# A four-layer network on one core: router weights held in TensorE, slot places made by POOL, and nine latent pieces a unit instead of eight

## The chip, the core and the metric

The kernel runs on one NeuronCore of a Trainium2 chip. The metric is the device time of one execution in microseconds (us); the figure for a kernel is the median of its runs. Engines are named as the profile names them: PE is TensorE (PEld its weight loads), DVE is VectorE, ACT is ScalarE, POOL is GpSimd, SP is SyncE, which here issues nearly all plain DMAs.

## The reference, cut to what matters

A network of four layers works on `x` of 4 x 512 tokens with 256 features, all in float32. Each layer normalises `x` and adds an attention part and a feed-forward part to it. The change touches layer 2 alone. Its attention part is a gated linear attention (16 heads); its feed-forward part is a small transformer block of its own: a latent attention, then a mixture of experts with one shared expert and seven routed ones, of which each token takes two.

```python
x = x + _L2_attn_ref(xn, ...) + _L2_ffn_ref(xn, ...)      # xn = layernorm(x)

def expert_ffn(x, wg, wu, wd):
    h = silu(x @ wg) * (x @ wu) / 8.0
    return h @ wd

def moe(x, sh_gate, sh_up, sh_down, r_gate, r_up, r_down, router_w, router_b):
    shared = expert_ffn(x, sh_gate, sh_up, sh_down)
    logits = x @ router_w + router_b                      # 256 -> 7
    probs = sigmoid(logits)
    scores, idx = top_k(probs, 2)
    scores = scores / sum(scores)
    w = sum(one_hot(idx, 7) * scores)
    return shared + sum over e of w[e] * expert_ffn(x, r_gate[e], r_up[e], r_down[e])

h = x + attention(rmsnorm(x, ln1_w), ...)                 # the latent attention
out = h + moe(rmsnorm(h, ln2_w), ...)
```

## The kernel before, in words

**Data.** The stream `x` and its normalised rows `xn` stay on the chip: 16 tiles of 128 tokens, 4 to a batch of 512. A batch transposed to features (two blocks of 128 features by 512 tokens) is made by `to_features`. A float32 product appears in the trace as two records on PE, a transpose as one.

**Who orders the instructions.** The program is written as generators that are advanced in turn, and a scheduler then fixes one order for each engine: it takes instructions by priority (their place in the written program) when its own estimates say that their inputs and buffers are ready, so neighbouring pieces are mixed. On the chip each engine runs its list in that order and waits at the first instruction whose inputs are not there. Pools give each tile name a number of buffers; an instruction that writes a new tile waits until the old user of the buffer has finished.

**Layer 2.** `layer2` runs 32 gated units (8 pairs of heads x 4 batches). `run(u, beside, rate)` advances three chains of one unit: `gated_unit` (scores `sc`, values `pt` with Wv, sums `st`, `pok`, the turned products `okt` and `pvt`, gates `pt` with Wg, the second scores, `pov`), `gated_supply` for the next unit (projections `pj` with Wk, Ws, Wq and the turned copies `turn`) and `gated_drain` for the unit before (`ot`, then `o` with Wo). After each of its 19 steps it adds `rate` to a credit that begins at zero in each call, and advances another chain, `beside`, once for every whole credit:

```python
credit = 0.0
for what in "mmmmsmsmmdmmsmsdmsd":
    next(chains[what], None)
    credit += rate
    while credit >= 1:
        credit -= 1
        next(beside, None)
```

For units 0 to 23 (`first` is 24) the chain beside is `latent_chain`, the whole latent attention and the router, at the rate `beside`. After unit 23 whatever is left of it is written in one go. For units 24 to 31 it is `routed2`, at the rate 1.25: the dispatch of tokens to experts, then 38 blocks of 128 rows through four stages (`fetch2`, `features2`, `hidden2`, `output2`).

**The latent chain** goes over 16 groups of heads (4 batches x 4) with three groups in flight: `latent_inputs` per batch, `latent_keys`, `latent_maxima` (scores `qk`, their maxima `mx`), `latent_va` per batch, `latent_values` (scores `kq`, exponentials `pr`, masks by POOL, `pv`, `pvt`), then per batch `latent_output` (`att`, `op`) and `experts2`.

**`experts2`** adds `h` to `x` on POOL (L1616), normalises it (squares on ACT, rsqrt on POOL, the scaling L1448 on DVE), transposes it to `a2T`, and computes the router's logits `lg`: for each of four tiles of tokens the 128 tokens are the stationary operand and the 7 columns of router weights stream by (L1626, two blocks of features), and the bias comes in as a product of a row of ones with the bias row (L1629). Then come the sigmoid (L1632), the two best by `top_weights`, their shares, and in the next piece the shared expert: `gu` (L1643), SiLU (L1646), the product (L1647), and `down` (L984).

**`dispatch`** turns the choices of all 2048 tokens into places. PE counts (`rank` L171, `count` L173); DVE makes each token's slots. The table from slot to token is built by PE: for each of 16 tiles and 2 choices, `place` (L239, 128x128, one where a lane equals the place inside the block) and `token` (L241, 128x38) are made, and `in_slot` (L244) accumulates `place` transposed times `token`. `place` and `token` have four buffers each. Then POOL gathers each block's rows by an indirect DMA (`r`, L294), SP loads the expert's weights `we`, and POOL sends the results back by an indirect DMA (`l_outs`, L334). The same `dispatch` serves layer 3.

**Around it on POOL.** The scaling of a gated unit's result `o` is three POOL instructions: a sum (L1301), a power (L1305) and the product in two halves (L1308). They stand in the same in-order list as the masks (L1558), the rsqrt steps (L377, L378) and the indirect DMAs.

Of the kernel before, what the change touches and what calls it, by code (L numbers as in the profile page):

```python
# [7 lines left out]
F32 = mybir.dt.float32  # L8
AF = mybir.ActivationFunctionType
ALU = mybir.AluOpType  # L10
# [3 lines left out]
P = 128  # L14
NB = 4
T = 512
D = 256
KD = D // P
NTILE = NB * T // P
EXT = 272  # L20
NEG = -3.0e38
# [16 lines left out]
def of_parity(ap, p):  # L38

    return ap.rearrange("q (j two) -> q two j", two=2)[:, p, :]  # L40
# [38 lines left out]
class Net:  # L79
# [78 lines left out]
    def dispatch(self, moe, rows, top, w, wk, pool, tag, keep=None):  # L158
# [3 lines left out]
        nc = self.nc  # L162
        ne, k, blocks = moe["ne"], moe["k"], moe["blocks"]
        cols = NTILE * ne
        tile = lambda name, *shape, dt=F32, of=wk: of.tile(list(shape), dt, tag=name, name=name, bufs=1)
# [62 lines left out]
        inside, first, less = tile("inside", P, NTILE, k), tile("first", P, NTILE, k), tile("less", P, NTILE)  # L228
# [6 lines left out]
        ps = pool.tile([P, blocks], F32, tag=tag, name="in_slot")  # L235
        for i in range(NTILE):
            for m in range(k):
                place = wk.tile([P, P], F32, tag="place", name="place", bufs=4)
                nc.vector.tensor_scalar(place, self.lane, inside[:, i, m : m + 1], None, ALU.is_equal)  # L239
                token = wk.tile([P, blocks], F32, tag="token", name="token", bufs=4)  # L240
                nc.vector.tensor_scalar(  # L241
                    token, self.starts[:, :blocks], first[:, i, m : m + 1], less[:, i : i + 1], ALU.is_equal, ALU.mult
                )
                nc.tensor.matmul(  # L244
                    ps, place, token, start=(i == m == 0), stop=(i == NTILE - 1 and m == k - 1)
                )
            if i % 2:
                yield
# [742 lines left out]
    def layer2(self):  # L991

        nc, a = self.nc, self.a
        UNITS = 8 * NB

        first, beside = 24, 0.44
        moe = self.moe2
        with ExitStack() as ctx:  # L1000
            tp = lambda n, bufs, **k: ctx.enter_context(self.tc.tile_pool(name=n, bufs=bufs, **k))
            self.gp = gp = {"wk": tp("ga", 1), "wk2": tp("ga2", 2), "ps": tp("gaps", 4, space=PSUM)}
            gp["gn"] = gn = gp["wk"].tile([P, 1], F32, tag="gn", name="gn")
            self.load(gn, a["l2_gn"])
            weights, units = self.weights, {}

            def supplied(u):
                pair, b = u // NB, u % NB
                for _ in norms[b]:
                    pass  # L1010
                if pair not in weights:
                    weights[pair] = self.gated_weights(pair)
                units[u] = {"b": b, "w": weights[pair]}
                return self.gated_supply(units[u])

            def normed(b):
                self.layer_norm(b)
                yield
                self.to_features(
                    gp["ps"], self.xn[:, 4 * b : 4 * b + 4, :], self.xnT[:, :, b * T : (b + 1) * T], tag="ps"  # L1020
                )
                yield

            def run(u, beside, rate):


                supply = supplied(u + 1) if u + 1 < UNITS else iter(())
                drain = self.gated_drain(units[u - 1]) if u else iter(())
                credit = 0.0
                chains = {"m": self.gated_unit(units[u]), "s": supply, "d": drain}  # L1030
# [7 lines that stand above are left out]
            norms = [normed(b) for b in range(NB)]  # L1038
            for it in (norms[0], supplied(0)):
                for _ in it:  # L1040
                    pass
            with ExitStack() as lctx:
                lp = self.lp
                lp["wk"] = lctx.enter_context(self.tc.tile_pool(name="la", bufs=1))
                lp["w"] = lctx.enter_context(self.tc.tile_pool(name="laps", bufs=4, space=PSUM))
                latent = self.latent_chain()
                for u in range(first):
                    run(u, latent, beside)
                for _ in latent:
                    pass  # L1050
            wk = tp("ex", 4)
            gp["ex"] = tp("exps", 4, space=PSUM)
            routed = self.routed2(wk)
            for u in range(first, UNITS):
                if u == UNITS - 1:
                    for _ in routed:
                        pass
                    self.collect(moe, wk)
                run(u, routed, 1.25)
            for _ in self.gated_drain(units[UNITS - 1]):  # L1060
                pass
        self.held.close()
# [280 lines left out]
    def latent_ahead(self, wp):  # L1343

        nc, a, NR = self.nc, self.a, 7
# [1 line left out]
        kvq, rk, up = tile("kvq", P, KD, P), tile("rk", P, KD, T), tile("up", P, 2, T)  # L1347
        vu, ow, ln1, shift_row = tile("vu", 64, D), tile("ow", P, KD, D), tile("ln1", P, D), tile("shift_row", P, 1)
        rotk, rotq = tile("rotk", P, T), tile("rotq", P, 2, T)
        rw, rb, ln2, sh = tile("rw", P, KD, NR), tile("rb", 1, NR), tile("ln2", P, D), tile("sh", P, 3, D)  # L1350
        kp = lambda ap: ap.rearrange("(k p) n -> p k n", p=P)
        self.load(kvq, kp(a["l2_kvq"]))
        self.load(ln1, a["l2_ln1"].partition_broadcast(P))
# [9 lines left out]
        self.load(ow, kp(a["l2_o_w"]))  # L1363
        self.load(shift_row, a["shift_row"])
        self.load(rw, kp(a["l2_rw"]))
        self.load(rb, a["l2_rb"])
        self.load(ln2, a["l2_ln2"].partition_broadcast(P))
        for q, n in enumerate(("gate", "up")):
            self.load(sh[:, q].rearrange("p (k i) -> p k i", k=KD), kp(a["l2_sh_" + n]))
# [238 lines left out]
    def experts2(self, b):  # L1608

        nc, lp = self.nc, self.lp  # L1610
        NR = 7
# [7 lines left out]
        aT = wk.tile([P, KD, T], F32, tag="a1", name="a2T")  # L1619
        self.to_features(pw, h, aT, tag="w")  # L1620
        yield
        ps = pw.tile([P, 4, NR], F32, tag="w", name="lg")
        for i in range(4):
            c, p = i // 2, i % 2
            for k in range(KD):
                nc.tensor.matmul(  # L1626
                    ps[:, i, :], of_parity(aT[:, k, c * D : (c + 1) * D], p), rw[:, k, :], start=(k == 0), stop=False
                )
            nc.tensor.matmul(ps[:, i, :], self.ones_row, rb, start=False, stop=True)  # L1629
        pr = self.small.tile([P, 4, NR + 6], F32, tag="pr", name="pr", bufs=2)  # L1630
        nc.gpsimd.memset(pr, NEG)
        nc.scalar.activation(pr[:, :, :NR], ps, AF.Sigmoid)  # L1632
        yield
        top, _ = self.top_weights(pr, NR, 2)
        nc.vector.tensor_copy(self.top2[:, 4 * b : 4 * b + 4, :NR], top)
        nc.vector.tensor_tensor(top, top, pr[:, :, :NR], ALU.mult)
        self.share(self.w2[:, 4 * b : 4 * b + 4, :NR], top)

        ps = []
        for q in range(2):  # L1640
# [5 lines left out]
        nc.scalar.activation(u, ps[0], AF.Silu)  # L1646
        nc.vector.scalar_tensor_tensor(u, ps[1], 1.0 / 8, u, ALU.mult, ALU.mult)  # L1647
        yield
        self.down(b, lambda cs: [u[:, cs]], [sh[:, 2, :]], None, pw, "w")
        yield  # L1650

# [255 lines left out]
```

## Time and profile before

| what | value |
| --- | --- |
| median of 3 runs | 2368.2 us (2363.25 to 2370.14) |
| the profiled execution | 2364.41 us, of which the span is 2362.7 us |
| PE / DVE / ACT / POOL busy | 2024.8 / 1249.7 / 831.7 / 622.3 us |
| chain that ended last, by engine | PE 61%, DVE 13%, issue 12%, DMA 7%, POOL 5% |
| layer 2, first gated unit to the first `sc` of unit 24 | 568 to 1560 us |
| dispatch of layer 2, `rank` to the last `in_slot` | 1597 to 1625 us |
| end of the last gated unit's last `o` (L1328) | 1916 us |

The profile is one execution. Busy shares are averages over stages that have different limits; the row of forty slices gives the busy share in tenths for 59 us each, and the row of the clock what PE was granted. A busy PE is not PE at its peak: records of matmuls overlap, and their ends are modelled. An idle time is put down to the one who ended it.

### The profile page before, as it was taken

What the parts mean: (1) busy time and instruction counts of PE and PEld (TensorE: products, weight loads), DVE (VectorE), ACT (ScalarE), POOL (GpSimd) and SP (SyncE); (2) the same over time, 40 slices, a digit from 0 to 9 for tenths busy, and PEclk for the clock granted to TensorE, in tenths of its full rate; (3) what the DMA queues carried; (4) which work ended last, traced back from release to release, by engine and by line L of the source; (5) the groups of instructions that cost most, each with busy time, mean ns of one, the idle gap of its engine ahead of it and who ended that gap; (6) DMA issues with size and microseconds to landing.
All of it is one profiled execution on the core that took longest, in us unless ns stands there. A gap on an engine that the chain in (4) does not pass through costs nothing.

```text
span 2362.7 us, 36356 instructions
## 1 busy us (share of the span) xinstructions
PE 2024.8 (86%) x13455; PEld 1500.8 (64%) x13455; DVE 1249.7 (53%) x3747; ACT 831.7 (35%) x1708; POOL 622.3 (26%) x725
## 2 busy tenths in 40 slices
PE   5754087876999999999999999999999868998985
PEld 2452076763666676666666676667788656777884
DVE  5755066658556655555556555637556575223222
ACT  1110056652334433434434333442444323333211
POOL 5324534443121211121121212112343231112221
PEclk9855599997999999999999999988999979999998
DMA  9911378873000000000000000003333305445675
GB/s 313 326 40 64 122 265 274 273 262 119 1 12 5 10 12 6 7 10 5 8 10 5 12 5 5 17 1 123 110 102 103 114 19 179 162 161 189 218 258 202
DMA packets 152537, 244.03 MB, mean 103 GB/s; under 512 B 15846, under 2 KB 111944, under 8 KB 152232
## 3 DMA queue, kind: packets, MB, share of 16 engines
q1 hardware_dynamic: 137336, 199.50, 25.9%
q0 software_dynamic: 15024, 42.20, 5.2%
q8 instruction: 107, 1.75, 0.3%
q14 instruction: 70, 0.57, 0.1%
HBM read 190.41 MB, written 66.58 MB: 109 GB/s over the span
## 4 chain that ended last, share of the span: by engine, by line
PE 61%; DVE 13%; issue 12%; DMA 7%; POOL 5%; ACT 2%; SPq 1%; POOLq 0%; another core or an unknown queue 0%; DVEq 0%; ACTq 0%
PE pt L1215 7%; PE pj L1137 6%; PE o L1328 4%; DMA r<-l_rows,in_slot 3%; PE g L1717 3%; PE kq L1550 3%; PE pov L1279 3%; PE sc L1200 2%; PE gu L958 2%; PE qk L1518 2%; PE o L1727 2%; DVE junk L1525 2%; PE pv L1566 2%; PE o L971 1%; POOL l_outs L334 1%
## 5 line engine op out<-in xcount | busy, mean ns | idle before, releaser
L334 POOL DMA_INDIRECT l_outs<-y,to x172 | 169.5, 986 | 383.6 <-ACT y L333 292.5
L1717 PE MATMUL g<-rT,we 128*128 128x128 f32 x1248 | 157.8, 285 | 8.0 <-ACT rT L327 7.7
L1717 PEld LDWEIGHTS g<-rT,we 128*128 128x128 f32 x1248 | 153.4, 200 | 15.4 <-ACT rT L327 12.5
L333 ACT ACTIVATE y<-o,share 128x256 f32<-128x256 f32 x172 | 80.9, 473 | 195.3 <-PE o L1727 108.3
L1525 DVE CUSTOM_DVE_ANT_0 junk<-qk,hide 128x512 f32<-128x512 f32 (+3 forms) x256 | 124.6, 487 | 43.5 <-PE qk L1518 24.9
L294 POOL DMA_INDIRECT r<-l_rows,in_slot x77 | 76.8, 998 | 244.8 <-PE rt L325 158.2
L306 DVE TENSOR_TENSOR mine<-r,number 128x2 f32<-128x2 f32 (+1 forms) x96 | 16.3, 170 | 227.0 <-DMA r<-l_rows,in_slot 164.3
L1558 POOL TENSOR_SCALAR_AFFINE_SELECT pr<-pr 128x512 f32<-128x512 f32 x64 | 40.2, 639 | 338.6 <-ACT pr L1555 338.6
L958 PE MATMUL gu<-rT,we 128*128 128x128 f32 x760 | 111.6, 286 | 19.3 <-issue 9.5
L1328 PE MATMUL o<-Wo,oT 128*128 128x256 f32 x512 | 125.2, 387 | 0.0
L1215 PE MATMUL pt<-Wg,xnT 128*128 128x256 f32 x512 | 123.2, 392 | 1.7 <-ACT oT L1322 0.7
L958 PEld LDWEIGHTS gu<-rT,we 128*128 128x128 f32 x760 | 103.5, 197 | 31.3 <-issue 15.2
L325 PE MATMUL rt<-ident,r 128*128 128x128 f32 x344 | 65.4, 296 | 67.6 <-DMA r<-l_rows 62.9
L1215 PE MATMUL pt<-Wv,xnT 128*128 128x256 f32 x512 | 120.1, 386 | 0.0
L1206 DVE TENSOR_TENSOR s<-sc,keep 128x512 f32<-128x512 f32 x128 | 82.4, 683 | 70.5 <-PE sc L1200 70.5
L1150 DVE RECIPROCAL rz<-rz 128x128 f32<-128x128 f32 x128 | 117.4, 935 | 0.4
L327 ACT COPY rT<-rt 128x256 f32<-128x256 f32 x172 | 61.4, 372 | 148.7 <-PE rt L325 79.4
L1215 PEld LDWEIGHTS pt<-Wg,xnT 128*128 128x128 f32 x512 | 96.3, 194 | 25.9 <-issue 7.1
L410 PE MATMUL tr<-ident,xn 128*128 128x128 f32 x160 | 34.2, 353 | 85.6 <-DVE xn L395 81.0
L1215 PEld LDWEIGHTS pt<-Wv,xnT 128*128 128x128 f32 x512 | 95.0, 191 | 14.9
L1555 ACT ACTIVATE pr<-kq 128x512 f32<-128x512 f32 (+1 forms) x192 | 86.2, 530 | 49.9 <-PE kq L1550 49.4
L1328 PEld LDWEIGHTS o<-Wo,oT 128*128 128x128 f32 x512 | 97.2, 200 | 8.7 <-ACT oT L1322 0.2
(455 smaller groups left out, 4505.2 us busy)
## 6 DMA issues: line engine op xcount, KB each, us to landing
we<-l_packed SPq DMA_DIRECT2D x133, 384.0 KB
we<-l_w SPq DMA_DIRECT2D x78, 512.0 KB
we<-l_wo SPq DMA_DIRECT2D x39, 512.0 KB
l_rows<-none SPq DMA_DIRECT2D x1, 12920.0 KB
r<-l_rows SPq DMA_DIRECT2D x19, 680.0 KB
xn<-l_outs SPq DMA_DIRECT2D x32, 256.0 KB
l_rows<-xn SPq DMA_DIRECT2D x8, 544.0 KB
l_packed<-l_w_gate SPq DMA_DIRECT2D x1, 4096.0 KB
```

Of the source, the lines that this page charges most:

```text
L294: self.nc.gpsimd.indirect_dma_start(out=r[:, m, :], out_offset=None, in_=moe["rows"][:, :], in_offset=bass.IndirectOffsetOnAxis(ap=moe["in ...
L333: nc.scalar.activation(y, ps, AF.Copy, scale=share)
L334: self.no_order(moe["name"] + " back", nc.gpsimd.indirect_dma_start(out=moe["outs"][:, :], out_offset=bass.IndirectOffsetOnAxis(ap=to, axi ...
L958: nc.tensor.matmul(ps[:, q, :], we[:, q, k * P : (k + 1) * P], rT[:, k, :], start=(k == 0), stop=(k == KD - 1))
L1137: nc.tensor.matmul(ps, w[n][:, k, :], self.xnT[:, k, t["b"] * T : (t["b"] + 1) * T], start=(k == 0), stop=(k == KD - 1))
L1150: inverse = lambda c: nc.vector.reciprocal(rz[:, c * P : (c + 1) * P], rz[:, c * P : (c + 1) * P])
L1206: nc.vector.tensor_tensor(s, ps[hh], keep4, ALU.mult)
L1215: nc.tensor.matmul(ps[:, i, :], self.xnT[:, k, s : s + P], w[n][:, k, :], start=(k == 0), stop=(k == KD - 1))
L1328: nc.tensor.matmul(ps[:, p, :], of_parity(oT[:, h, c * D : (c + 1) * D], p), wo[:, h, :], start=(h == 0), stop=(h == 1),)
L1525: nc.vector.tensor_tensor_reduce(out=junk[:, :m], in0=tiles[j][:, off : off + m], in1=self.hide[:, T - m :], op0=ALU.add, op1=ALU.max, sca ...
L1555: nc.scalar.activation(pr[:, j, off : off + m], tiles[j][:, :m], AF.Exp, scale=0.25)
L1717: nc.tensor.matmul(pt[:, m, :], we[:, q, k * T + m * P : k * T + (m + 1) * P], rT[:, k, :], start=(k == 0), stop=(k == KD - 1),)
```

## The change

Four things are done, all in layer 2.

1. In `layer2` the rate of the latent chain beside units 0 to 23 goes from 0.44 to 0.475.
2. In `experts2` the router's logits are computed with the router weights as the stationary operand: `lgT` has 7 rows and 512 token columns. ACT copies it out of PSUM and adds the bias, which for that is loaded as a column of 7 instead of a row. Four transposes then bring it back to tokens by 7.
3. The pieces of `experts2` are cut anew: the logits now stand in one piece with the shared expert's `gu`, SiLU and product; transposes and sigmoid are the next piece; the choice of the two best stands with `down`. There are five pieces as before.
4. In `dispatch`, `place` is made by POOL for layer 2. Layer 3's stays on DVE.

```diff
         for i in range(NTILE):
             for m in range(k):
                 place = wk.tile([P, P], F32, tag="place", name="place", bufs=4)
-                nc.vector.tensor_scalar(place, self.lane, inside[:, i, m : m + 1], None, ALU.is_equal)
+                (nc.gpsimd if moe is self.moe2 else nc.vector).tensor_scalar(place, self.lane, inside[:, i, m : m + 1], None, ALU.is_equal)
...
-        first, beside = 24, 0.44
+        first, beside = 24, 0.475
...
-        rw, rb, ln2, sh = tile("rw", P, KD, NR), tile("rb", 1, NR), tile("ln2", P, D), tile("sh", P, 3, D)
+        rw, rb, ln2, sh = tile("rw", P, KD, NR), tile("rb", NR, 1), tile("ln2", P, D), tile("sh", P, 3, D)
...
-        self.load(rb, a["l2_rb"])
+        self.load(rb, a["l2_rb"].rearrange("o n -> n o"))
...
-        ps = pw.tile([P, 4, NR], F32, tag="w", name="lg")
-        for i in range(4):
-            c, p = i // 2, i % 2
-            for k in range(KD):
-                nc.tensor.matmul(
-                    ps[:, i, :], of_parity(aT[:, k, c * D : (c + 1) * D], p), rw[:, k, :], start=(k == 0), stop=False
-                )
-            nc.tensor.matmul(ps[:, i, :], self.ones_row, rb, start=False, stop=True)
-        pr = self.small.tile([P, 4, NR + 6], F32, tag="pr", name="pr", bufs=2)
-        nc.gpsimd.memset(pr, NEG)
-        nc.scalar.activation(pr[:, :, :NR], ps, AF.Sigmoid)
-        yield
-        top, _ = self.top_weights(pr, NR, 2)
-        nc.vector.tensor_copy(self.top2[:, 4 * b : 4 * b + 4, :NR], top)
-        nc.vector.tensor_tensor(top, top, pr[:, :, :NR], ALU.mult)
-        self.share(self.w2[:, 4 * b : 4 * b + 4, :NR], top)
+        ps = pw.tile([NR, T], F32, tag="w", name="lgT")
+        for k in range(KD):
+            nc.tensor.matmul(ps, rw[:, k, :], aT[:, k, :], start=(k == 0), stop=(k == KD - 1))
+        lg = wk.tile([NR, T], F32, tag="q1", name="lgT")
+        nc.scalar.activation(lg, ps, AF.Identity, bias=rb)

         ps = []
         for q in range(2):
...
         nc.scalar.activation(u, ps[0], AF.Silu)
         nc.vector.scalar_tensor_tensor(u, ps[1], 1.0 / 8, u, ALU.mult, ALU.mult)
         yield
+        ps = pw.tile([P, 4, NR], F32, tag="w", name="lg")
+        for i in range(4):
+            c, p = i // 2, i % 2
+            nc.tensor.transpose(ps[:, i, :], of_parity(lg[:, c * D : (c + 1) * D], p), self.ident[:NR, :NR])
+        pr = self.small.tile([P, 4, NR + 6], F32, tag="pr", name="pr", bufs=2)
+        nc.gpsimd.memset(pr, NEG)
+        nc.scalar.activation(pr[:, :, :NR], ps, AF.Sigmoid)
+        yield
+        top, _ = self.top_weights(pr, NR, 2)
+        nc.vector.tensor_copy(self.top2[:, 4 * b : 4 * b + 4, :NR], top)
+        nc.vector.tensor_tensor(top, top, pr[:, :, :NR], ALU.mult)
+        self.share(self.w2[:, 4 * b : 4 * b + 4, :NR], top)
         self.down(b, lambda cs: [u[:, cs]], [sh[:, 2, :]], None, pw, "w")
         yield
```

`lgT` in SBUF takes the buffer `q1`, which the keys (`latent_keys`) and the maxima (`latent_maxima`) use too.

## The prediction

> **What bounds the kernel now.** I began with the page: the busy shares, the forty slices, and the clock granted to PE.
>
> ```profile
> span 2362.7 us, 36356 instructions
> PE 2024.8 (86%) x13455; PEld 1500.8 (64%) x13455; DVE 1249.7 (53%) x3747; ACT 831.7 (35%) x1708; POOL 622.3 (26%) x725
> PE   5754087876999999999999999999999868998985
> PEclk9855599997999999999999999988999979999998
> ```
>
> From slice 10 to slice 31 PE is full, and this is the gated layer; no other engine is. So within the layer a change is worth what it takes from PE: its work, its idle time, and its time at a lower clock. The dip of the clock row in slices 26 and 27 (1536 to 1654 us) is where the change acts. The second view is the table of stretches (width, then busy time of PE, PEld, DVE, ACT, POOL, then granted clock, DMA share, GB/s).
>
> ```profile
> 570.00:1540.00 970.00, 960.68 (x6636) 651.11 (x6635) 570.53 (x1354) 383.89 (x709) 161.41 (x184) 0.98 0.03 8
> 1540.00:1560.00 20.00, 16.99 (x131) 10.58 (x129) 6.98 (x18) 6.08 (x15) 6.31 (x8) 0.91 0.00 1
> 1560.00:1576.00 16.00, 16.00 (x93) 11.24 (x92) 3.34 (x6) 7.37 (x19) 2.68 (x4) 0.79 0.00 0
> 1576.00:1592.00 16.00, 14.48 (x59) 8.63 (x57) 4.69 (x26) 7.47 (x13) 2.74 (x3) 0.79 0.00 1
> 1592.00:1608.00 16.00, 14.75 (x93) 10.38 (x92) 12.92 (x53) 5.59 (x9) 0.37 (x3) 1.00 0.00 1
> 1608.00:1626.00 18.00, 16.86 (x92) 14.53 (x92) 15.98 (x74) 0.59 (x1) 0.31 (x1) 0.78 0.37 125
> 1626.00:1644.00 18.00, 15.34 (x93) 13.46 (x94) 10.83 (x47) 4.75 (x12) 11.39 (x12) 0.78 0.56 180
> 1700.00:1800.00 100.00, 99.19 (x710) 81.01 (x709) 60.40 (x185) 47.11 (x99) 42.75 (x44) 1.00 0.34 104
> ```
>
> The 970 us before 1540 lose 1% to idle PE and 2% to the clock; so nearly does the stretch after 1700. Between them lies the seam: the latent pieces left over after unit 23, then the dispatch of layer 2. There PE idles 9.6 us in 104 (3.0 + 0 + 1.5 + 1.3 + 1.1 + 2.7) and the clock falls. The third view says who was waited for in the seam (total us, times, longest), and two rows of PE in order of time say what the lower clock costs: the same 32 matmuls take 2.36 us at clock 1.00 and 4.14 us at 0.50, a ratio of 1.75.
>
> ```profile
> PE o L1106 <- DVE h L1101: 2.3, 1, 2.3
> PE pv L1566 <- POOL pr L1558: 2.3, 1, 2.3
> PE tr L410 <- DVE xn L1448: 1.5, 1, 1.5
> ```
>
> ```profile
> 1511.59 2.36 PE L1566 MATMUL pv<-pr,va 128*32 128x512 f32 x32
> 1563.24 4.14 PE L1566 MATMUL pv<-pr,va 128*32 128x512 f32 x32
> ```
>
> The last view is the rows of single lines (min/median/max ns), from which the moved operations are priced.
>
> ```profile
> L239 DVE TENSOR_SCALAR place<-lane,inside x32: 278/282/290, 1608.7 to 1623.8; 128x128 f32<-128x128 f32 x32
> L241 DVE TENSOR_SCALAR token<-starts,first,less x32: 297/299/302, 1608.3 to 1624.0; 128x38 f32<-128x38 f32 x32
> L1558 POOL TENSOR_SCALAR_AFFINE_SELECT pr<-pr x64: 633/634/798, 638.6 to 1563.8; 128x512 f32<-128x512 f32 x64
> L377 POOL TENSOR_SCALAR rms<-ms x8: 193/193/487, 545.4 to 1577.6; 128x4 f32<-128x4 f32 x8
> L1305 POOL TENSOR_TENSOR rs<-rs,neghalf x32: 1633/1644/1674, 611.7 to 1907.9; 128x8 f32<-128x8 f32 x32
> ```
>
> **The rate 0.44 to 0.475.** The latent chain has 208 pieces (12 inputs, 16 keys, 64 maxima, 4 va, 80 values, 12 outputs, 20 router and shared expert). The credit starts at zero in every unit, so 19 steps give floor(8.36) = 8 pieces now and floor(9.025) = 9 after. 24 units place 192 now; 16 are left, and they are the last values, the output and the whole router of batch 3, each waiting for the one before it. With 9 a unit, 207 are placed by unit 22 and the last one in unit 23. In the built program's order the last shared expert's `o` moves from the middle of unit 24 to the start of unit 23, and from the first matmuls of unit 25 on PE's order is the same, instruction for instruction. So the whole effect is how soon PE comes to unit 25.
>
> What can be had: idle 9.6 less the usual 1% (1.0) is 8.6 us. The clock: 20 x 0.09 + 32 x 0.21 + 36 x 0.22 = 16.4 us of (1 - clock), so 33 us at half, less the usual 2% of 104 us (4 at half): 29 x (1 - 1/1.75) = 12.3 us. Together 20.9.
>
> What stays: units 23 and 24 now run with little beside them. Two gated units are 55 us of PE (about 27.6 each, summing one unit's rows), and with shared `o`, rank, count, in_slot and two expert blocks some 75. The stretch 1592:1608 shows such a lone unit: 1.25 us idle in 16, so 5.9 in 75, less 0.7 usual, 5.2. One fall of the clock, 6.8 us long like that of 1560 to 1567, is 2.9. The second `op` of batch 3 stands only 4.3 us of PE ahead of the transposes `tr`, while add, squares, rsqrt and scale need about 5.7 (0.7 + 2.5 + 1.2 + 0.4 and handovers): a wait of 1.5, already counted within the 5.2. So 8 stays, from 3 to 20.9.
>
> The clock can be read in two ways. In this trace it fell to 0.50 at 1560 though PE had idled only 0.3 us since 1554, and at 1622 in a run of narrow matmuls with no gap at all; I therefore count the clock as tied to how full PE's work is, and the seam's loss as recoverable. The Trainium skill, "TensorE: Matmul & The Clock Gate", in "Why this matters for your kernels", ties a fall to idle gaps over about 3 us. No gap in the seam is that long (the longest is 2.4 us), so by that rule the seam should not have lost its clock, and the gain from clock would be zero and not 12.3.
>
> **The router.** Now 12 products per batch: 24 records of 128x7 (859.45 to 862.93 us, 3.5 us of PE), each bound by its weight load of 0.19 us. After: two products of 512 columns, four records like `pj` (1.98 us), and four transposes (0.6 us, like the four of `okt`): 2.5 us. Saved 1.0 x 4 = 4 us. ACT gets one more pass of 128x512 size, 0.6 us x 4, at 41% load; its chain (matmul, ACT, transpose, sigmoid) is longer, but `rank` stands some 15 us of PE behind the last transposes. The Sigmoid's table load stays. The bias tile is one DMA at 126 us in place of another, used 480 us later: nothing. Putting the router behind the shared expert keeps five pieces per batch: nothing by itself.
>
> **The places on POOL.** 32 `place` leave DVE, about 0.2 us each in its pipeline, 6.6 us. No row shows this operation on POOL. Ends: 0.19 (L377, 128x4) and 1.64 us (L1305, the slow power). I take 0.3, between L377 and the 128x512 select at 0.63, since the size lies between and the kind is L377's. POOL's order is four places, unit 23's three-step scaling of `o` (3.9 us), then 28 places, then the gathers of rows, which need all 32 anyway. The `token`s wait for buffers that `in_slot` frees, and behind them on DVE stand `ke`, `ok`, `mx` of unit 24, for which PE waits: a slow POOL would stop all three. The cover: among the 28 places' matmuls PE has 9.6 us of unit 24 (`st` 0.57, `pj` 1.98 twice, `pok` 1.96, `okt` 0.66, `st` 0.88, `ot` 1.09, part of `Wg` 0.46) and 28 x 0.39 = 10.9 of its own `in_slot` work: 20.5 us. At 0.3 POOL needs 8.4, all hidden; PE pays from 20.5 / 28 = 0.73 us per place. The fifth place comes about 13.6 us after the end of the `sc` before it (dispatch ops on DVE 5.0, `o` and `ms` 2.5, POOL 4.2, products 1.6, one place) and PE asks for it after about 13.8: 0 to 2 us late, I take 0. As PE's `in_slot` is bound by its weight loads (64 x 0.19 = 12.3 us) the relief of DVE gains PE nothing: 0.
>
> The rule against this move is in the Trainium skill, "SBUF — State Buffer", "Who interferes with whom": a DVE `tensor_scalar` in its two-port mode and a POOL instruction lock each other out. No row before shows such a pair. If each place waited for a token, it would cost an estimated 0.6 us, 16.8 in all, still under the cover, and the sum would not change.
>
> **Sum.** 20.9 + 4.0 - 8.0 = 16.9, taken as 17 us. The profiled execution took 2364.4 us (span 2362.7), so 2347; it lies 3.8 below the median of the runs, 2368.2, so the median after is 2351.
>
> **Rivals.** (A) The seam only moves. Units 23 and 24 lose as the stretch 1626:1644 does: 0.148 idle per us and clock 0.78. Over 75 us that is 11.1 + 33 x (1 - 1/1.75) = 25 us, as much as is removed: about 2368. For it: a dispatch inside a lone unit is the same in both. Against: 1592:1608 lost no clock, and the `in_slot` matmuls are now mixed with wide ones. (B) Slower: POOL's places are slow. At L1305's 1.64 us they take 45.9, which is 25.4 over the cover: net +8.5, 2377. It decides from (20.5 + 17) / 28 = 1.34 us per place. Against: only the power has such a row. (C) The change doesn't do what it says: nine pieces a unit make PE wait for DVE more often than the seam did (now 5.9 us in 13 waits of `kq` for `mx`); four times that takes the gain away, 2369. Against: DVE is at 59%.
>
> **How the numbers follow.** My case 0.74, A 0.15, B 0.07, C 0.04. About 0.3% (7 us, so 2361 and 2375) is what a measurement of this kernel can tell from no change. My case lies below 2361, with an eighth of A: faster 0.76; the rest of A and half of C: 0.15; B and half of C: 0.09. My case alone: from 24.9 (nothing stays) to 8 us of gain, 2343 to 2360. The range adds 5 us below, for runs as far below the median as the fastest shown, and reaches above into A: 2338 to 2366.
>
> **What would show it.** Right: clock near 1.00 and idle under 8 us between the last `att` (L1593) and unit 25; `lgT` of about 2 us; `place` on POOL under 0.73 us with no wait of `in_slot` for it; unit 25 some 17 us earlier and all later stages moved as a block. Wrong: the fall of the clock found again around `in_slot`; DVE idle for buffers of `token`; PE's idle between 570 and 1540 risen by more than 10 us.

## The result, and the profile after

The kernels before and after were compared in 20 runs each. After takes 2370.4 us (median), before 2375.3; the ratio of after to before is 0.9986, 95% interval 0.9969 to 1.0004. Three to five microseconds, not clear of zero, came out of a forecast of 17. The kernel before itself has medians between 2358 and 2375 us on the chips used here, so in what follows only ratios on one chip, and parts of a trace, are compared.

The page of the profiled execution of after, the rows of PE as before (the span is 2383.4 us):

```profile
PE 2036.2 (85%) x13391; PEld 1504.8 (63%) x13391; DVE 1248.7 (52%) x3715; ACT 835.8 (35%) x1711; POOL 642.5 (27%) x757
PE   6654178865999999999999999999999879998985
PEclk9855599997999999999999999999999977999997
```

The dip of the clock row that stood in slices 26 and 27 is gone: the seam was closed as forecast. But PE's busy time rose by 11 us, though the router now takes less of it. The stretches say where (columns as before: width, busy PE, PEld, DVE, ACT, POOL, clock, DMA):

```profile
574.00:1535.00 961.00, 941.55 (x6343) 627.87 (x6345) 548.44 (x1327) 376.70 (x698) 159.03 (x184) 0.97 0.02 7
...
1600.00:1620.00 20.00, 18.02 (x128) 14.89 (x126) 17.16 (x64) 3.54 (x7) 13.43 (x21) 1.00 0.34 113
1620.00:1640.00 20.00, 18.85 (x136) 14.48 (x135) 13.88 (x39) 7.68 (x12) 12.40 (x19) 1.00 0.18 55
```

From 1540 to 1640, with all of the dispatch in it, the clock is 1.00. The loss stands ahead of it, in the weave, as the units with the latent chain beside them are called from here on: in 961 us of it PE idles 19.5 us, where 970 us of before had 9.3. The waits of PE in 574 to 1655 (total us, times, longest) name most of it:

```profile
PE kq L1550 <- DVE mx L1525: 10.8, 18, 2.4
PE pt L1215 <- DVE pv L1254: 3.1, 4, 1.0
```

The same wait in before (565 to 1680):

```profile
PE kq L1550 <- DVE mx L1525: 5.9, 13, 1.6
```

The scores `kq` waited for the maxima 13 times before (5.9 us) and 18 times now. That was rival C. These waits are 4.9 of the 11 us of new idle time; the gates `pt`, which wait for `pv`, add 2.7 (0.4 before). And idle time is only half of the loss. One row of the `qk` matmuls by shape (count, covered time, which is the time with at least one of them on PE, mean ns of one, idle before them), of before and then of after, shows equal count and equal mean but more time covered; the other three shapes of `qk` rise too (18.3 to 20.5, 11.4 to 14.0 and 9.4 to 11.9 us):

```profile
L1518 PE MATMUL qk<-kT,q 32*128 32x384 f32 x128 | 21.2, 533 | 0.3 <-DVE mx L1525 0.3
```

```profile
L1518 PE MATMUL qk<-kT,q 32*128 32x384 f32 x128 | 25.3, 533 | 0.0
```

The four matmuls of a score piece use 32 rows of the array each, and run side by side when all four PSUM banks are free; when the banks come free one after the other they start one after the other. No row of waits shows that time, for PE counts as busy. Two `qk` pieces of the same 16 records in after, in order of time, are such a pair: 1.15 us, and 2.26 us beside the exponentials (ACT, 807.19 to 809.25) that empty its banks.

```profile
762.01 1.15 PE L1518 MATMUL qk<-kT,q 32*128 32x384 f32 x16
808.17 2.26 PE L1518 MATMUL qk<-kT,q 32*128 32x384 f32 x16
```

In the first piece the four heads start within 0.02 us. In the second they start 0.15, 0.49 and 0.49 us apart, the last three each 0.05 us after an exponential has ended. Before has such pieces too, but fewer: 5 of the 16 `qk` pieces of this kind cover over 1.5 us there, 10 in after.

The Trainium skill, "TensorE: Matmul & The Clock Gate", "Part 3: Packing small matmuls — row/col tiling", says that matmuls in different row groups overlap; the fast piece agrees (1.15 us), and the slow one shows what the overlap needs here.

**The account.** The stage from the first `sc` of unit 0 to the first `sc` of unit 26 holds the same work in both kernels, but for the router. It took 1112.8 us in the profile of before, 1119.5 in a second one, 1119.4 in after. Against the second one, whose clock was lower in the weave too, the gains are: idle in the seam (from unit 22 on) 12.3 to 8.9, 3.4 us; time at half clock (granted clock 0.50) there 34 to 0, at the 1.75 of the prediction 14.6 us; the router's rows 16.8 to 10.3, 6.5 us. Together 24.5. The losses: idle in the weave (units 0 to 21) 8.2 to 19.4, 11.3 us; covered time of `qk`, `kq` and `pv` 183.8 to 196.0, 12.2 us; clock in the weave (45.5 to 51.6 us at half) 2.6. Together 26.1. The stage should be 1.6 longer and is 0.1 shorter. The clock's part of the loss is the least certain. In the weave the three executions with the rate 0.475 (after, a_again and rate_only below) spent 48 to 57 us at half clock, the five with eight pieces at the old places 19 to 46; between the means, 52.1 and 30.6, lie 21.5 us, which at 1.75 is 9.2 us rather than 2.6. Why the clock falls there was not tested.

### The profile page after: what moved, and what is told of

It is laid out like the page before. It is cut to its first block, busy times and chain, and to the rows that moved or that the text cites. A ratio compares the mean times of both kernels' runs of the same rounds, so it can differ in the third digit from the quotient of the medians.

```text
span 2383.4 us, 36271 instructions
## 1 busy us (share of the span) xinstructions
PE 2036.2 (85%) x13391; PEld 1504.8 (63%) x13391; DVE 1248.7 (52%) x3715; ACT 835.8 (35%) x1711; POOL 642.5 (27%) x757
## 3 DMA queue, kind: packets, MB, share of 16 engines
q8 instruction: 107, 1.75, 0.3%
## 4 chain that ended last, share of the span: by engine, by line
PE 61%; DVE 12%; issue 11%; DMA 5%; SPq 4%; POOL 4%; ACT 2%; another core or an unknown queue 0%; POOLq 0%; DVEq 0%; ACTq 0%
PE pt L1215 8%; PE pj L1137 6%; SPq L356 4%; PE o L1328 4%; PE g L1718 4%; PE kq L1550 3%; PE gu L958 3%; DMA r<-l_rows,in_slot 3%; PE sc L1200 2%; PE pov L1279 2%; PE o L1728 2%; PE qk L1518 2%; PE o L971 2%; PE pv L1566 2%; DVE junk L1525 1%
## 5 line engine op out<-in xcount | busy, mean ns | idle before, releaser
L1718 PE MATMUL g<-rT,we 128*128 128x128 f32 x1248 | 161.9, 289 | 7.8 <-ACT rT L327 7.8
L1328 PE MATMUL o<-Wo,oT 128*128 128x256 f32 x512 | 131.8, 403 | 0.0
L1328 PEld LDWEIGHTS o<-Wo,oT 128*128 128x128 f32 x512 | 101.0, 207 | 18.3 <-issue 4.0
L1555 ACT ACTIVATE pr<-kq 128x512 f32<-128x512 f32 (+1 forms) x192 | 86.9, 530 | 54.9 <-PE kq L1550 54.6
```

Of the source, the lines that this page charges most:

```text
L1328: nc.tensor.matmul(ps[:, p, :], of_parity(oT[:, h, c * D : (c + 1) * D], p), wo[:, h, :], start=(h == 0), stop=(h == 1),)
L1555: nc.scalar.activation(pr[:, j, off : off + m], tiles[j][:, :m], AF.Exp, scale=0.25)
L1718: nc.tensor.matmul(pt[:, m, :], we[:, q, k * T + m * P : k * T + (m + 1) * P], rT[:, k, :], start=(k == 0), stop=(k == KD - 1),)
```

## The experiments

All are from the same two sources. Idle is PE's in 575 to 1495 us (920 us less busy time); the next column is the covered time of `qk`, `kq` and `pv` up to unit 26; the stage is that of the account. "Short" counts how often the gated PE work between a `qk` piece and the `kq` piece behind it is under 2 us, in 575 to 1495 of the trace.

| kernel | pieces a unit, placed | idle us | qk+kq+pv us | short | stage us | ratio to before (95%) |
| --- | --- | --- | --- | --- | --- | --- |
| before; b_again | 8, credit | 8.8; 8.8 | 183.1; 183.8 | 0; 0 | 1112.8; 1119.5 | 1 |
| after; a_again | 9, credit | 19.5; 19.4 | 196.0; 196.0 | 9; 9 | 1119.4; 1120.0 | 0.9986; 0.9998 (0.9979–1.0017) |
| rate_only | 9, credit | 19.5 | 197.9 | 9 | 1130.3 | 1.0049 (1.0032–1.0066) |
| rest_only | 8, credit | 9.0 | 183.8 | 0 | 1108.2 | 0.9973 (0.9955–0.9991) |
| router_only | 8, credit | 9.0 | 183.6 | 0 | 1111.9 | 0.9997 (0.9982–1.0011) |
| pool_only | 8, credit | 8.9 | 183.2 | 0 | 1116.5 | 0.9999 (0.9985–1.0013) |
| even | 8.67, carried | 25.3 | 182.5 | 7 | 1114.0 | 0.9993 (0.9976–1.0009) |
| placed9; again | 9, fixed steps | 11.1; 11.1 | 182.9; 183.5 | 5; 5 | 1100.8; 1103.7 | 0.9901 (0.9881–0.9922); 0.9935 (0.9917–0.9954) |
| short8 | 8, fixed steps | 19.2 | 204.3 | 9 | 1144.5 | 1.0138 (1.0116–1.0160) |
| placed_only; again | 9, fixed steps | 11.1; 11.0 | 183.8; 183.9 | 5; 5 | 1119.8; 1119.8 | 1.0006 (0.9994–1.0018); 1.0015 (0.9998–1.0033) |
| banks_a | 9, credit | 33.1 | 172.9 | 9 | 1130.6 | 1.0109 (1.0089–1.0129) |
| first26 | 8, credit | 9.1 | 177.3 | 0 | – | 0.9935 (0.9912–0.9958) |

### The parts of the change

b_again and a_again are the two kernels unchanged; rate_only is before with 0.475, rest_only after with 0.44, router_only before with the new `experts2`, pool_only before with the places on POOL. Each is a part of the diff shown above, for instance

```diff
-  first, beside = 24, 0.44      # rate_only, from before
+  first, beside = 24, 0.475
```

> The kernel before once more, for a second profile: how far the stage from the first gated unit to unit 25 varies between executions (1066.9 us in the first profile, 9.4 us of idle PE before the seam). Theory W (weave: nine latent pieces a unit bring PE to the score matmuls before DVE has read the PSUM banks of the last ones, so PE waits and the four row groups no longer run side by side): again 1067 +- 6 us, idle in the weave 8 to 11, and `kq` waits for `mx` under 7 us. Theory N (noise: the profiled execution of the changed kernel was a bad one): the stage moves by 10 us or more between executions of one kernel.

> The changed kernel once more. W: the stage from the first gated unit to unit 25 again takes 1070 to 1085 us, with 18 to 23 us of idle PE before 1540, `kq` waiting for `mx` 9 to 12 us, and `qk` busy 70 us or more instead of 60; the time within 0.4% of before. N: that stage is shorter than before's by 10 to 17 us in this execution, and the time is 10 us or more below before's or lost behind unit 25.

> The kernel before with the rate 0.475 alone. W: the seam is gone (PE full and clock 1.00 around the last `att`), but the weave has the idle time of the changed kernel (18 to 23 us before 1540) and `qk` busy 70 us or more: time within 6 us of before, 3 to 5 us above the changed kernel (its router is missing). Theory P (POOL's places, 0.6 us each, eat the gain): 8 us or more faster than the changed kernel, since no place is on POOL. N: 13 to 17 us faster than before.

> The changed kernel with the rate 0.44: router and POOL's places alone. W: idle in the weave back at 8 to 11 us and `qk` busy 60 us, the seam of 16 late pieces is back with its falls of the clock; time 2 to 6 us below before, from the router. P: slower than before by 3 to 8 us, as POOL's places stand bare in the seam. N: 3 to 5 us below before.

> The kernel before with the router part alone (rate 0.44, places on DVE). If the 4 us that the prediction gave to the router are right and the places on POOL are worth nothing: 3 to 6 us below before, and within 3 us of the kernel with router and places (1108 us for the stage, 0.27% below before). If the places on POOL bring part of that: no more than 2 us below before.

> The kernel before with the places on POOL and nothing else. The prediction put this at zero: place 0.6 us each on POOL (as in after), hidden, ratio 0.998 to 1.002, unit 24 to unit 26 within 3 us of before's 125. Rival: taking 32 places off DVE, which is busy 0.9 of the time during in_slot, makes in_slot faster: then this part is what rest_only (0.9973) has over router_only (0.9997), ratio 0.996 to 0.998.

The idle time and the lost overlap in the weave belong to the rate and to nothing else: rate_only has 19.5 us of idle like after, rest_only and router_only 9.0. They come back alike in each of the executions, so they are no accident of one profile. The rate alone makes the kernel 0.3 to 0.7% slower, where its term of the sum was a gain of 12.9 us. The places on POOL are worth nothing by themselves, as forecast; the router's 4 us (0.17%) lie inside its interval. Together, in rest_only, they gain 0.27%, which is clear of zero; rest_only also has the least time at half clock in the weave (19 us, for 27 to 46 in the other four with eight pieces), and whether its gain is more than that is open.

### Slow readers or few banks?

half_a and half_b are after and before with half of the columns of each maximum left out; the exponentials are scaled so that they stay finite:

```diff
-  out=junk[:, :m], in0=tiles[j][:, off : off + m], in1=self.hide[:, T - m :],
+  out=junk[:, : m // 2], in0=tiles[j][:, off : off + m // 2], in1=self.hide[:, T - m : T - m // 2],
...
-  nc.scalar.activation(pr[:, j, off : off + m], tiles[j][:, :m], AF.Exp, scale=0.25)
+  nc.scalar.activation(pr[:, j, off : off + m], tiles[j][:, :m], AF.Exp, scale=0.0001)
```

> The changed kernel with each maximum of the latent scores taken over the first half of its columns only (DVE's 256 instructions of L1525 shrink from about 490 to 300 ns), and the exponentials scaled to stay finite; all else as it was, and PE's order nearly so. Theory W (PE comes to the score matmuls before DVE has read their PSUM banks): the wait of `kq` for `mx` falls from 10.8 us to under 5, `qk` + `kq` + `pv` are busy 184 to 188 us instead of 196, idle PE in the weave falls from 19 to under 13, and the stage from the first gated unit to unit 26 falls from 1120 to 1095 to 1107 us. Theory R (the denser weave costs PE through its clock or through the order of matmuls alone, not through DVE): the stage stays within 5 us of 1120.

> The kernel before with the same halved maxima. W: less to free here, since its wait of `kq` for `mx` is 5.9 us and its `qk` + `kq` + `pv` 183: the stage falls from 1113 to 1119 us to 1105 to 1113, so less than half as much as in the changed kernel. R: no change of the stage in either.

The mean maximum took 0.32 us for 0.49. If DVE were simply too slow for nine pieces, the difference of the two would shrink with the reading. It did not: idle 15.9 against 5.0 us, covered time 178.4 against 161.9, stage 1097.9 against 1088.4. Neither theory fits: the stage of after came out as W said, but its idle (15.9 for under 13) and its wait of `kq` for `mx` (6.6 us for under 5) did not, and before, which W expected to gain less than half as much, gained 24 to 31 us where after gained 22. half2_a and half2_b halve ACT's reading as well:

```diff
-  pr = wk.tile([P, 4, 1280], F32, tag="pr", name="pr")
+  pr = lp["pr"]          # one buffer, set to one at the start
...
-  nc.scalar.activation(pr[:, j, off : off + m], tiles[j][:, :m], ...)
+  nc.scalar.activation(pr[:, j, off : off + m // 2], tiles[j][:, : m // 2], ...)
```

> Half_a with ACT's share halved too: the exponentials pr read only the first half of each PSUM bank's columns and write half of their row; the row itself is one buffer, set to one at the start (what is left out of the computation: half the columns of the maxima and of the exponentials). Halving DVE's reading alone did not take away the difference between the two rates (nine less eight pieces: weave idle +11.1 us, busy time of qk, kq and pv +16.5 us, unit 0 to unit 26 +9.5 us). Theory B (four PSUM banks): qk and kq share four banks, so the next piece's matmuls wait, bank by bank, until DVE has read the maxima out of them or ACT the exponentials; nine pieces a unit leave less time for that round trip. By B, with both readers halved, the difference against half2_b falls to at most 4 us of idle and 7 us of busy time (3 of these are three pv groups that the written order splits, 1.05 us each). Theory R (order alone: the denser weave puts the instructions in a worse order, whoever reads the banks): the differences stay as in half_a against half_b, 9 to 16 us of busy time and over 8 of idle.

> The kernel before with the same two halvings (left out: half the columns of the maxima and of the exponentials): the other side of the comparison. Both theories expect weave idle of about 4 us and 155 to 162 us of qk, kq and pv; only the distance to half2_a tells them apart.

Idle 18.3 against 5.0, covered time 168.9 against 156.0, stage 1087.5 against 1076.8. By its own bounds theory B falls here too, and R's hold (13.3 us of idle, 12.9 of covered time): only `qk` came closer (64.0 and 54.4 in half_a and half_b, 54.9 and 51.6 here), while the distance of `kq` grew from 5.2 to 7.3. The longest wait in total of half2_a, then of half2_b, in 571 to 1496:

```profile
PE kq L1550 <- DVE mx L1525: 6.7, 11, 2.5
```

```profile
PE kq L1550 <- DVE mx L1525: 2.0, 2, 1.5
```

With maxima that take a third less time, `kq` still waits 11 times, up to 2.5 us. That speaks for the reader's turn, more than its speed, as what is late. banks_a asks it from the other side:

```diff
-  self.gp = gp = {..., "ps": tp("gaps", 4, space=PSUM)}
+  self.gp = gp = {..., "ps": tp("gaps", 3, space=PSUM)}
...
-  lp["w"] = lctx.enter_context(self.tc.tile_pool(name="laps", bufs=4, space=PSUM))
+  lp["w"] = lctx.enter_context(self.tc.tile_pool(name="laps", bufs=5, space=PSUM))
```

> After, with five PSUM banks for the latent chain and three for the gated unit instead of four and four. B: with a fifth bank the first matmuls of the next piece need not wait, kq's waits for mx fall from 10.8 us to under 5 and the busy time of qk, kq and pv from 196 to under 190 us; the gated unit's own waits rise (it has three buffers for sc, pt, st), by an amount that no row shows; if by less than 10 us the kernel becomes faster than after by 0.3%. R: waits and busy time of qk, kq and pv stay within 3 us, and the gated unit's waits come on top: slower than after.

```profile
PE ot L1321 <- DVE pv L1254: 15.0, 9, 2.6
PE pt L1215 <- DVE s L1206: 5.4, 3, 2.3
PE kq L1550 <- DVE mx L1525: 4.1, 5, 1.8
```

Here B's numbers held, and R's did not: `kq` waits 4.1 us and the covered time falls to 172.9. So the loss at the scores needs both, the four shared banks and an order that leaves the reader late; but a bank taken from the gated unit costs it more (15.0 and 5.4 us in the rows above), and the kernel is 1.1% slower.

### Where the pieces stand

One place of after, on PE and on DVE in order of time, shows the turn being lost:

```profile
901.46 1.15 PE L1518 MATMUL qk<-kT,q 32*128 32x384 f32 x16
902.54 0.66 PE L1248 MATMUL okt<-ident,ok 128*128 128x128 f32 x4
903.13 0.88 PE L1188 MATMUL st<-v,eT 128*64 128x128 f32 x12
903.93 0.33 PE L1321 MATMUL ot<-ident,o 128*128 128x128 f32 x1
906.66 1.13 PE L1550 MATMUL kq<-q,kT 32*128 32x384 f32 x4 [2.40 <-DVE mx L1525]
```

```profile
902.96 1.23 DVE L1149 TENSOR_TENSOR_SCAN rz<-one_col,eF 128x512 f32<-128x512 f32 x1 [0.70 <-ACT eF L1148]
904.22 0.95 DVE L1150 RECIPROCAL rz<-rz 128x128 f32<-128x128 f32 x1
905.09 0.50 DVE L1525 CUSTOM_DVE_ANT_0 junk<-qk,hide 128x384 f32<-128x384 f32 x1
...
905.51 0.95 DVE L1150 RECIPROCAL rz<-rz 128x128 f32<-128x128 f32 x1
906.37 0.23 DVE L1525 CUSTOM_DVE_ANT_0 junk<-qk,hide 128x128 f32<-128x128 f32 x1
...
906.52 0.69 DVE L1252 TENSOR_REDUCE mx<-okt 128x8 f32<-128x512 f32 x1
```

`qk` is done at 902.6; PE has 1.7 us of other work and stands at `kq`. DVE begins the first maximum at 905.09, behind a scan and a reciprocal of the gated unit that come first in its order. It then puts a reciprocal of 0.95 us between the two maxima of the first bank, for which `kq` waits until 906.6, and a reduction of 0.69 us ahead of the second bank's.

The credit decides where this can happen. 0.44 puts the eight pieces behind steps 3, 5, 7, 10, 12, 14, 16, 19; 0.475 puts nine behind 3, 5, 7, 9, 11, 13, 15, 17, 19. In the trace of after `okt` and `st` (with at most one `ot`) stand alone between `qk` and `kq` four times and `sc` and `turn` five times (1.3 to 1.7 us); before has no such place. These are the short covers, a cover being the gated work of PE between the two. Of the 10.8 us that `kq` waits for `mx` in after, 6.3 stand behind six of the nine short covers, and the same in a_again and rate_only. First the credit was carried over from unit to unit (8.67 pieces on average, so that the places rotate):

```diff
-  first, beside = 24, 0.475
+  first, beside = 24, 208 / 456 + 1e-6
...
-  credit = 0.0
+  credit = carry[0] if u < first else 0.0
...
+  carry[0] = credit
```

> The changed kernel, but the credit is carried from unit to unit, at 208 pieces in 456 steps: eight or nine pieces a unit, none left after unit 23. If the loss grows with the number of pieces a unit (W by density): between the two, a seam without falls of the clock, idle in the weave 12 to 17 us, stage 1105 to 1115 us, time 0.1 to 0.5% below before. If it hangs on where in the unit the pieces fall (W by place): idle in the weave can be anywhere from 5 to 25 us; then single units should show waits of `kq` for `mx` at particular steps.

That gained nothing: with seven short covers it idles 25.3 us, though its covered time is not longer than that of before, so idle time and lost overlap do not always come together. Then placed9 and short8 took the count and the places apart; both replace the credit by a string of marks:

```diff
-  for what in "mmmmsmsmmdmmsmsdmsd":
+  for n, what in enumerate("mmmmsmsmmdmmsmsdmsd"):
-      credit += rate
+      credit += int(rate[n]) if isinstance(rate, str) else rate
...
-  first, beside = 24, 0.475
+  first, beside = 24, "0110101001010101001"     # placed9, from after
+  first, beside = 24, "0010101010001010101"     # short8, from rest_only (0.44)
```

> After, with the nine pieces of a unit put behind fixed steps (2, 3, 5, 7, 10, 12, 14, 16, 19) instead of where the credit of 0.475 puts them (3, 5, 7, 9, 11, 13, 15, 17, 19): the places of the kernel before and one more behind step 2. Theory S (short covers: the loss comes from pairs of pieces with under 2 us of gated PE work between a qk piece and the kq piece behind it, 9 of 43 after, none before and none here): the weave's idle is 8 to 11 us (19.4 after), kq waits for mx 5 to 7 us (10.8), busy time of qk, kq and pv 183 to 188 us (196.0), and with the seam closed as in after, unit 0 to unit 26 takes 1094 to 1104 us (1119.7) and the ratio is 0.991 to 0.995. Theory D (density: nine pieces are too many for four banks wherever they stand): idle over 16, busy time over 193, ratio 0.998 or more.

> Rest_only (eight pieces a unit, router and places as after) with its pieces behind steps 3, 5, 7, 9, 13, 15, 17, 19, so that okt and st, or sc and turn, again stand alone between pieces, 11 times in all, while a unit still has only eight. S: the loss of after comes back at the lower density: weave idle 16 to 24 us (8.2 in rest_only), busy time of qk, kq and pv 193 to 200 us (183.8), unit 0 to unit 26 1125 to 1135 us (1108.2), ratio 1.004 to 1.008. D: as rest_only, idle under 11, ratio 0.996 to 0.999.

```profile
575.00:1495.00 920.00, 908.88 (x6219) 600.43 (x6215) 539.59 (x1311) 361.76 (x677) 156.06 (x180) 0.98 0.03 7
```

```profile
575.00:1495.00 920.00, 900.81 (x6096) 610.65 (x6095) 531.27 (x1246) 361.93 (x664) 152.56 (x174) 0.98 0.03 7
```

The first row is the second run of placed9, the other one short8. Theory S held on both sides in idle and covered time: nine pieces at the old places and one new one idle 11.1 us, wait for `mx` 6.2 us and cover 183 us; eight pieces behind eight of the nine steps of after idle 19.2 and cover 204, and 6.4 of the 10.0 us that `kq` waits for `mx` in short8 stand behind short covers. D is out: it is not how many pieces, but behind which steps, and what order the scheduler makes of that. short8 cost more than S said (1.4% for 0.4 to 0.8). And length alone is not the condition: placed9, for which S had counted no short cover, has five of 1.8 to 1.9 us, all a `pt`, and no wait for `mx` at them, while in after `kq` waits 0.4 to 0.65 us behind each of six covers of 2.3 us (`turn` and `o`) before it starts, and behind none of the five in before. What DVE has in its order ahead of the maxima counts as well; which of the nine places costs how much was not measured.

### What the closed seam is worth alone

placed_only is before with placed9's string and nothing else; then both were run again on one chip.

> The kernel before with nothing changed but the places of the pieces: nine a unit behind steps 2, 3, 5, 7, 10, 12, 14, 16, 19. By S this is the seam's gain alone, without the weave's loss: the prediction's term was 20.9 less 8.0, so 12.9 us, ratio 0.9946; with what router and places gave together in rest_only (0.9973) it would have to make placed9's 0.9901, so 0.9928; expected 0.991 to 0.996, weave idle 8 to 12 us, unit 0 to unit 26 within 4 us of placed9's 1100.8 plus the router's 4. By D it would be rate_only's 1.0049 again.

> placed9 unchanged, beside placed_only on one chip. If the gain belongs to the kernel, the ratio is again 0.988 to 0.993 on this chip, weave idle 11 us, qk, kq and pv 183 us. If the chip made it, the ratio lies near placed_only's, within 0.3%.

> placed_only unchanged. If the difference belongs to the kernel, the ratio is again 0.999 to 1.002 and the clock falls again for some 25 us in the in_slot matmuls of the seam, where placed9 loses about half of that; if the chip made it, the ratio is 0.991 to 0.996.

My expectation fell: placed_only gains nothing, twice, and its difference from placed9 belongs to the kernel and not to the chip. Its weave is as good as placed9's (11.0 us of idle). What it lacks is clock in the seam: from unit 22 to 26 it has 34 us at half clock in both runs, as before had, where placed9 has 13.7 and 23.9. In the dispatch itself the second runs differ little: placed_only is at half clock for 27.3 us, placed9 for 23.9, and placed_only's other 6.8 us lie ahead of it, from 1544 us on. One stretch of the dispatch, placed_only's second run and then placed9's, shows both near half clock:

```profile
1590.00:1610.00 20.00, 18.66 (x73) 13.32 (x73) 10.29 (x39) 1.41 (x4) 1.91 (x2) 0.56 0.33 111
```

```profile
1590.00:1610.00 20.00, 20.00 (x91) 15.32 (x90) 7.69 (x24) 2.67 (x4) 11.85 (x21) 0.50 0.17 57
```

Clock (about 4 to 9 us), idle in the seam (2.5) and the weave with the shorter router (5 us) make up 12 to 16 of the 16 to 19 us between the two stages. Whether router or places decide it when the pieces stand well is open: pool_only and router_only, which gain nothing, had the old steps. Neither is needed for a seam at full clock: rate_only, which has neither, was at half clock there for only 6.8 us.

first26 closes the seam in a third way: rest_only with the latent chain beside 26 units of eight pieces.

```diff
-  first, beside = 24, 0.44
+  first, beside = 26, 0.44
...
-  run(u, routed, 1.25)
+  run(u, routed, 1.67)
```

> Rest_only (router and places as after, eight pieces a unit) with the latent chain beside 26 units instead of 24, so that 26 x 8 = 208 places the whole chain without a denser weave; the routed experts then run beside six units, at 1.67 for 1.25. If only the density of the weave cost what the closed seam gave, the weave keeps its idle of 8.2 us, the seam's 10.6 us idle and 41 us at half clock mostly go, and the ratio to before is 0.988 to 0.994. Rival: the dispatch and the routed blocks, beside fewer units, now lose what the seam lost (1.67 is a third denser): ratio 0.997 to 1.003.

It came out at the upper end of the first forecast. The weave keeps its idle, 1540 to 1640 runs at clock 1.00, and part is given back later: from 1700 to 1800 PE is busy 94.7 us of 100, where before had 99.2.

**The best version** is placed9, after with the nine pieces behind fixed steps: 0.7 and 1.0% faster than before in its two comparisons, where after as it was given is between 0.3% faster and the same. first26, at 0.65%, is not told apart from its second comparison.

## Why the prediction was wrong, point by point

- **The rate, the step that failed.** "So the whole effect is how soon PE comes to unit 25" was right as a sentence and wrong as a sum: the term counted the seam (20.9 less 8) and put the price of the ninth piece in the weave at zero. It measured 11 us of idle, 12 us of lost overlap and 3 to 9 us of clock, with rate_only slower by 0.49% for a forecast 0.55% gain. The prediction had the rule that gives the steps, counted the pieces with it (8 now, 9 after), and did not ask behind which steps they fall. Nor does the term come out where that price is not paid: placed_only, with a good weave, gains nothing.
- **Rival C** was the right mechanism at 0.04. It was priced by the waits of `kq` for `mx` alone and needed them four times; they rose 1.8 times. The other half stood in no row of waits, since a piece whose four matmuls run one after the other is busy time. "DVE at 59%" spoke against it, and is no argument: in the place shown DVE was late by its order, and with a third less work in the maxima the waits stayed.
- **Seam and clock.** In after both went as forecast: clock 1.00 from 1540 to 1640, idle in 1540 to 1660 7.3 us. Rival A is refuted there. But placed_only lost 34 us at half clock in the same seam, so the 12.3 us were no sure term; the prediction had a single execution to size it from.
- **Router.** Forecast 2.5 us a batch, measured (7.7 + 2.6) / 4 = 2.6. The rows of before add up to 4.2 a batch and not 3.5, so 6.5 us of PE were saved for 4 forecast; the ratio alone can't show either. The reading "each bound by its weight load of 0.19 us" does not come out of the trace: the 24 records (16 of them 128x7, 8 of the bias row) took 3.5 us, so their loads of 0.18 to 0.20 us overlap: after the first they start 0.11 to 0.21 us apart.
- **Places on POOL.** `place` took 0.60 us, twice what I assumed, but stays under the cover of 0.73, and `in_slot` waited 0.4 us for it. Cost about zero, as said; rival B is out. The lock that the Trainium skill ("SBUF — State Buffer", "Who interferes with whom") describes would show as 0.3 us more on a place or a token; beside places the tokens took 0.30 to 0.50 us, and the median token is 34 ns longer than before (rows below). But two tokens stood beside the two halves of POOL's product `o` (L1308): they took 1.08 us each and ended 0.04 us after the half beside them, as such a lock would make it, and `in_slot` waited 1.65 us for the first. The prediction had priced a lock between place and token alone. Such a long token needs no place on POOL: in rate_only one token beside that product took 1.03 us, and the other 31 at most 0.30.
- **The sign named as wrong** in the prediction, PE's idle between 570 and 1540 up by more than 10 us, is what happened.

The two rows of after (ns min/median/max, first and last start), and the first long token with what stood beside it and what waited for it:

```profile
L239 POOL TENSOR_SCALAR place<-lane,inside x32: 597/599/653, 1606.0 to 1629.4; 128x128 f32<-128x128 f32 x32
L241 DVE TENSOR_SCALAR token<-starts,first,less x32: 290/333/1086, 1605.8 to 1630.5; 128x38 f32<-128x38 f32 x32
```

```profile
1610.62 1.09 DVE L241 TENSOR_SCALAR token<-starts,first,less 128x38 f32<-128x38 f32 x1
1610.63 1.04 POOL L1308 TENSOR_TENSOR o<-o,rs 128x512 f32<-128x512 f32 x1
1611.86 0.39 PE L244 MATMUL in_slot<-token,place 128*128 128x38 f32 x2 [1.65 <-DVE token L241]
```

## What to carry to other kernels

When a chain is advanced beside another at a rate, ask behind which steps each piece falls, and what then stands between a matmul that fills PSUM banks and the next one that needs them: a count that fits better can land on worse places, and the same change with better places gained 0.7 to 1.0% where it had gained 0 to 0.1%. An engine's mean load alone does not say whether its in-order list gets to the one read in time. And look for lost overlap in the covered time of matmuls with equal counts and equal mean durations, for no wait shows it.

## What the runs showed of the hardware

- PE's clock can stay at 0.50 over 20 us in which PE is busy, by the profile, for all 20 (the second run of placed9 above, narrow `in_slot` matmuls among `pt`), while in after the same loop, with 2 us of idle in 20, ran at 1.00. The Trainium skill's rule in "TensorE: Matmul & The Clock Gate", "Why this matters for your kernels", ties a fall to gaps over about 3 us; no gap of that length stands in these stretches or in the 10 us ahead of them (the longest wait of PE there is below 2 us).
- The same program differs from chip to chip by up to 17 us (medians of before 2357.8 and 2375.1), and two executions of it by 13 us of half clock in the stage of the account (66.5 and 79.6).
- The comparison of a 128x128 tile takes 0.60 us on POOL, 0.28 on DVE.
- A DVE instruction of 0.30 us took 1.08 us beside a POOL product of 1.04 us, twice, and ended 0.04 us after it.
